# LoRA-conditioned projection and routed LoRA FFN: the setup's order of loads, copies and constant passes, and the banks of the last tile

## The chip, the cores and the metric

The kernel runs on one core of a Trainium2 chip. The metric is the device time of one execution in microseconds (us). The core's engines are TensorE (PE in the profile, its weight loads PEld), VectorE (DVE), ScalarE (ACT), GpSimd (POOL) and SyncE (SP), which in this kernel only issues DMAs.

## The reference

All data are float32. x is 8 batches of 512 rows of 2048. Each batch has an adapter (itok, one of 32) of rank 16. The result is x plus a routed low-rank FFN of a conditioned projection of x:

```python
# conditioned projection, per batch b
base_out = jnp.einsum('bti,oi->bto', x, W) + b
lora_h = jnp.einsum('bti,bir->btr', x, lora_As[adapter_mapping])
lora_out = jnp.einsum('btr,bro->bto', lora_h, lora_Bs[adapter_mapping])
y = base_out + lora_out * 2.0
# FFN: one of 8 experts per row, the one with the largest logit
logits = jnp.einsum('bsd,ed->bse', y, route_w)
topk_v, topk_idx = jax.lax.top_k(logits, 1)
route_weight = jax.nn.one_hot(topk_idx[..., 0], 8) * topk_v
h = jnp.einsum('bsd,erd->bser', y, A)
out = jnp.einsum('bser,eor->bso', route_weight[..., None] * h, Bw)
return x + out
```

W is 2048 by 2048 (16 MB in float32), x 32 MB, each batch's adapter two matrices of 16 by 2048.

## The kernel before

The projection y is never formed. What the FFN needs of y are 136 numbers a row (8 experts of rank 16, and 8 logits), so the kernel first folds W into the 136 columns `proj` (A and route_w side by side) and then applies the folded matrix to x. It has two stages.

**Setup.** W comes in 16 tiles of 128 output rows (1 MB each, `load_w`, four buffers), and proj in parts (`load_pj`). For each tile, `chunk_w` rearranges it into two halves `wv` of eight 128-column blocks: ScalarE copies the first half, VectorE the second (line 281). Each half has two buffers. Then `load_w(oc + 4)` is issued into the tile's buffer. `fold_w` adds the tile's 16 products into six PSUM banks `pc` (line 292): 16 float32 matmuls, each of which is two passes in the trace. After the last tile, ScalarE and VectorE alternately copy the banks to `cm` (line 302).

Beside the fold the setup makes the low-rank parts. `load_adapters` (line 159) works out the rows of each batch's adapters with small VectorE operations and fetches them through GpSimd's queue: `ad_b` (1 MB, one indirect DMA), `ad_ar` (1 MB, four indirect DMAs) and the bias. `turn_adapters` transposes `ad_b` on TensorE in four groups, ScalarE copies each (line 320); `turn` transposes `ad_ar` on VectorE (line 234); `fold_bias` forms the bias products on VectorE; `project_bias` and `project_adapters` are small matmuls, and the latter sends its result to DRAM and reads it back in four DMAs into `g4`.

The first unit of x (two tiles of 128 rows, 2 MB, `load_x`) is rearranged by `shuffle` into `xq` in 16 copies of 32 partitions (line 249): ScalarE makes four and GpSimd twelve. VectorE then transposes it in 32 by 32 blocks into `xT` (`turn_x`, line 234), and `heads` (line 400) can begin.

Before any of this, twelve matmuls on a constant tile `warm` run on TensorE (line 131). They read `warm` after a one-column ScalarE copy within the same tile (line 128), which in turn follows ScalarE's table load.

**Tile loop.** 32 tiles of 128 rows. In each half step n, TensorE does half of a tile's `heads`, and two of the four 512-column products of an earlier tile (`delta`, line 466). In between come `add_low` (the adapter's and the bias's part, line 424) and `turn_heads` (a transpose, line 455). VectorE does `route` (the choice of the expert, lines 437 to 445), `turn_low`, the next tile's transposes and `add_delta` (x plus the product, in place, line 478), after which SyncE stores the rows. ScalarE copies `whT` and seven of a unit's sixteen copies, GpSimd the rest.

The PSUM pools of the loop are `ps_h` (two tiles `ph`, 152 columns each), `ps_o` (two tiles `po` of two banks each) and `ps_s` (two).

**What sets the order.** The order on every engine is the order in which the program issues its instructions; the loop over `oc` (line 348) and the loop over n (line 509) write it out by hand. All loads and stores of W, proj, ffn_b and x stand in SyncE's queue, in program order, and a DMA in it that waits holds up those behind it.

Of the kernel before, what the change touches and what calls it, by code (L numbers as in the profile page):

```python
# [9 lines left out]
F32 = mybir.dt.float32  # L10
# [8 lines left out]
def kernel(  # L19
# [29 lines left out]
    nc = tc.nc  # L49
# [34 lines left out]

    warm = const.tile([P, P], F32, name="warm")
    nc.vector.memset(warm, 1.0)


    it_i = const.tile([P, B], I32, name="it_i")
# [27 lines left out]
    def load_x(u):  # L117
        xt = xpools[u % XB].tile([P, TPU, D], F32, tag=f"x{u % XB}", name=f"x_{u}")
        for k in range(TPU):
            b, r = divmod(TPU * u + k, TPB)  # L120
            nc.sync.dma_start(out=xt[:, k, :], in_=x[b, ts(r, P), :])
        x_tiles[u] = xt
# [2 lines left out]
    ident = const.tile([P, P], F32, name="ident")  # L125
    make_identity(nc, ident)

    nc.scalar.copy(warm[:, 1:2], warm[:, :1])
    pm = ps_s.tile([P, P], F32, tag="s", name="pm")
    for _ in range(12):  # L130
        nc.tensor.matmul(pm, warm, warm, start=True, stop=True)

    own_i = const.tile([P, B], I32, name="own_i")
# [22 lines left out]
    fb = const.tile([P, D], F32, name="fb")  # L156
    bias_o = const.tile([P, NO], F32, name="bias_o")

    def load_adapters():

        it_f = const.tile([P, B], F32, name="it_f")
        nc.vector.tensor_scalar(it_f, it_i, float(R), None, ALU.mult)
        row_f = const.tile([P, B], F32, name="row_f")
        nc.vector.tensor_tensor(row_f, it_f, own, ALU.add)
        nc.vector.tensor_tensor(row_f, row_f, mask, ALU.mult)
        brow_f = const.tile([P, 1], F32, name="brow_f")
        nc.vector.tensor_reduce(brow_f, row_f, AX.X, ALU.add)
        brow_i = const.tile([P, 1], I32, name="brow_i")
        nc.vector.tensor_copy(brow_i, brow_f)
        nc.gpsimd.indirect_dma_start(  # L170
            out=ad_b,
            out_offset=None,
            in_=cond_b,
            in_offset=bass.IndirectOffsetOnAxis(ap=brow_i, axis=0),
        )

        quad = const.tile([P, B], F32, name="quad")
        nc.vector.tensor_copy(quad, quad_i.rearrange("p i h -> p (i h)"))
        nc.vector.tensor_tensor(quad, quad, mask, ALU.mult)
        base = const.tile([P, 1], F32, name="base")  # L180
        nc.vector.tensor_reduce(base, quad, AX.X, ALU.add)
        odd = const.tile([P, 1], F32, name="odd")
        nc.vector.tensor_reduce(
            odd, mask.rearrange("p (i h) -> p h i", h=2)[:, 1, :], AX.X, ALU.add
        )
        it_q = const.tile([P, NQ, 2], F32, name="it_q")
        nc.vector.tensor_scalar(
            it_q, it_f.rearrange("p (k h) -> p k h", h=2), float(NQ), None, ALU.mult
        )
        arow_f = const.tile([P, NQ], F32, name="arow_f")  # L190
        nc.vector.tensor_tensor(arow_f, it_q[:, :, 1], it_q[:, :, 0], ALU.subtract)
        nc.vector.tensor_scalar(arow_f, arow_f, odd, base, ALU.mult, ALU.add)
        nc.vector.tensor_tensor(arow_f, arow_f, it_q[:, :, 0], ALU.add)
        arow_i = const.tile([P, NQ], I32, name="arow_i")
        nc.vector.tensor_copy(arow_i, arow_f)
        for m in range(NQ):
            nc.gpsimd.indirect_dma_start(
                out=ad_ar[:, m, :],
                out_offset=None,
                in_=cond_a.rearrange("s (i d) -> (s i) d", i=NQ),  # L200
                in_offset=bass.IndirectOffsetOnAxis(ap=arow_i[:, m : m + 1], axis=0),
            )
        nc.gpsimd.dma_start(out=bias_o, in_=bias)

    one = const.tile([P, NQ, Q], F32, name="one")
    own4 = const.tile([P, NQ], F32, name="own4")
# [25 lines left out]
    def turn(dst, src, h):  # L232

        nc.vector.transpose(  # L234
            dst[:, ts(h, HJ), :].rearrange("p j (g t) -> p g j t", t=Q),
            src.rearrange("p g (j a) -> p g j a", a=Q)[:, :, ts(h, HJ), :],
        )
# [69 lines left out]
    def fold_bias(js):  # L307
        for j in js:
            if j == 0:
                nc.vector.tensor_scalar(bp, pj[:, 0, :], bias_o[:, :1], None, ALU.mult)  # L310
            else:
                nc.vector.scalar_tensor_tensor(
                    bp, pj[:, j, :], bias_o[:, j : j + 1], bp, ALU.mult, ALU.add
                )

    def turn_adapters(g):
        pt = ps_s.tile([P, 4, P], F32, tag="s", name=f"pbT_{g}")
        for k in range(4):
            nc.tensor.transpose(pt[:, k, :], ad_b[:, ts(4 * g + k, P)], ident)
        nc.scalar.copy(ad_bT[:, ts(g, 4), :], pt)  # L320
# [27 lines left out]
    for oc in range(NO):  # L348
        if oc + 1 < NO:
            chunk_w(oc + 1)  # L350
        fold_w(oc)
        if oc == 2:
            load_adapters()
            fill_constants()
        if oc == 6:
            nc.sync.dma_start(out=fb, in_=ffn_b)
        if oc in (8, 10):
            load_x((oc - 8) // 2)
        if 6 <= oc < 10:
            turn_adapters(oc - 6)  # L360
        if oc in (7, 8):
            turn(ad_aT, ad_ar, oc - 7)
        if oc in (9, 10):
            fold_bias(range(8 * (oc - 9), 8 * (oc - 8)))
        if oc == 11:
            project_bias()
            project_adapters()
        if oc == 12:
            load_x(2)
            shuffle(0, moves[:4], nc.scalar.copy)  # L370
            shuffle(0, moves[4:], nc.gpsimd.tensor_copy)
        if oc == 13:
            for b in range(2):
                nc.scalar.copy(cm[:, :, ds(b * NA, R)], ad_aT[:, :, ts(b, R)])
        if oc == 14:
            for h in range(2):
                turn_x(0, h)
# [17 lines left out]
    def heads(t, j0, j1):  # L395
        s = batch_of(t) % 2
        if j0 == 0:
            ph_tiles[t] = ps_h.tile([P, NA], F32, tag="h", name=f"ph_{t}")
        for j in range(j0, j1):
            nc.tensor.matmul(  # L400
                ph_tiles[t],
                xT_tiles[t][:, j, :],
                cm[:, j, ds(s * R, NA)],
                start=(j == 0),
                stop=(j == NJ - 1),
            )
# [54 lines left out]

    def delta(t, h):

        po = ps_o.tile([P, HN, 512], F32, tag="o", name=f"po_{t}_{h}")
        for k in range(HN):
            nc.tensor.matmul(  # L466
                po[:, k, :], whT_tiles[t], fb[:, ts(h * HN + k, 512)], start=True, stop=True
            )
        po_tiles[t, h] = po

    def add_delta(t, h, parts=1):
        u, k = divmod(t, TPU)
        po = po_tiles.pop((t, h)).rearrange("p n d -> p (n d)")
        n = D // 2 // parts
        for m in range(parts):
            cols = ds(h * D // 2 + m * n, n)
            xs = x_tiles[u][:, k, cols]
            nc.vector.tensor_tensor(xs, xs, po[:, ts(m, n)], ALU.add)  # L478
            if t == NT - 1:
                store(t, cols)  # L480
        if t == NT - 2:
            store(t, ts(h, D // 2))
        elif t < NT - 2 and h == 1:
            store(t, ds(0, D))
# [24 lines left out]
    for n in range(2 * NT + 4):  # L509
        t, h = divmod(n, 2)  # L510
        if t < NT:

            if n == 3:
                heads(t, HJ, HJ + HJ // 2)
                turn_heads(0)
                heads(t, HJ + HJ // 2, NJ)
            else:
                heads(t, h * HJ, (h + 1) * HJ)
            if n == 2:
                add_low(0)  # L520
        if h == 0 and 0 < t <= NT:
            route(t - 1)
        tp, hp = piece(n - 1)
        if tp >= 0:
            add_delta(tp, hp, HN if tp == NT - 1 else 1)
        turn_x(t + 1, h)
        if h == 1 and 0 < t <= NT:
            keep_heads(t - 1)
        u, ms = shuffle_slot(n)
        shuffle(u, ms, nc.gpsimd.tensor_copy if n == 2 else nc.scalar.copy)  # L530
        if h == 1 and t < NT:
            turn_low(t)
        if piece(n)[0] >= 0:
            delta(*piece(n))
        if h == 1 and 0 < t < NT:
            add_low(t)
        if h == 1 and t < NT:
            b, k = divmod(t, TPB)
            if k == 0 and 0 < b < B - 1:
                nc.gpsimd.tensor_copy(  # L540
                    cm[:, :, ds((b + 1) % 2 * NA, R)], ad_aT[:, :, ts(b + 1, R)]
                )
        if h == 0 and 1 < t <= NT:
            turn_heads(t - 1)
        tq, hq = piece(n - 5)
        u, k = divmod(tq, TPU)
        if tq >= 0 and hq == 1 and k == TPU - 1 and u + XB < NU:
            load_x(u + XB)
# [48 lines left out]
```

## Time and profile before

| What | Value |
|---|---|
| median of 3 runs | 338.13 us (338.06 to 338.48) |
| profiled execution, own time | 338.08 us |
| its span, first to last instruction | 336.3 us |
| mean granted TensorE clock | 0.996 |
| TensorE busy | 324.2 us (96%) |
| VectorE busy | 232.3 us (69%) |
| ScalarE busy | 169.7 us (50%) |
| GpSimd busy | 138.1 us (41%) |
| DMA | 88.83 MB, 264 GB/s over the span |
| tile loop's first matmul | 75.58 us |

In a line of the timeline the first number is the start in us from the span's start, the second the time until the merged group's end; then come engine, line of the kernel, operation, output and inputs, and the count; in brackets the idle time of the engine before it, and what ended it. In a line of the chain of waits there are start, length and the work. In a line of the stretches, the stretch is followed by its length, then busy time and count of PE, PEld, DVE, ACT and POOL, then granted clock, the busy share of the DMA engines, and GB/s.

### The profile page before, as it was taken

Reading aid. Unit: us, or ns where it says so; the run is one execution under the profiler, and the core shown is the slowest. Engines: PE = TensorE matmul, PEld = TensorE weight load, DVE = VectorE, ACT = ScalarE, POOL = GpSimd, SP = SyncE. Lnnn points to the kernel's source line nnn. Section 1 sums busy time; section 2 is a strip of 40 time slices with the busy share of each in tenths; the row PEclk is TensorE's granted clock in tenths of the full one; section 3 lists DMA queues with packets and bytes.
Section 4 is the critical chain, followed back from the end, with each engine's and each line's share of the span. In section 5 each row is a group of like instructions: output and inputs, shape, how many; then the busy total and the mean of one; then the engine's idle time right before and its main releaser. Section 6 shows DMA issues by size and latency. Waiting matters only on the chain.

```text
span 336.3 us, 5099 instructions
## 1 busy us (share of the span) xinstructions
PE 324.2 (96%) x1962; PEld 259.9 (77%) x1962; DVE 232.3 (69%) x421; ACT 169.7 (50%) x193; POOL 138.1 (41%) x145
## 2 busy tenths in 40 slices
PE   6998999999999999999999999999999999999993
PEld 6898999998777777777777777777777777777751
DVE  1151464255887877787878787877877787877753
ACT  3222433625757566576647565757566575730000
POOL 2050001999981807182616455344708081700000
PEclk9999999999999999999999999999999999999998
DMA  7999999869333394949485766759494949333336
GB/s 218 401 405 411 413 417 420 333 239 399 147 128 139 126 370 196 385 153 383 141 359 179 323 223 276 264 239 342 172 374 170 377 160 385 146 125 127 126 125 250
DMA packets 15656, 88.83 MB, mean 264 GB/s; under 512 B 1664, under 2 KB 4368, under 8 KB 5392
## 3 DMA queue, kind: packets, MB, share of 16 engines
q1 hardware_dynamic: 14960, 86.33, 65.4%
q0 software_dynamic: 528, 2.11, 1.9%
q8 instruction: 15, 0.25, 0.3%
q10 hardware_dynamic: 144, 0.07, 0.1%
q14 instruction: 9, 0.07, 0.1%
HBM read 54.88 MB, written 33.62 MB: 263 GB/s over the span
## 4 chain that ended last, share of the span: by engine, by line
PE 77%; DMA 12%; POOL 4%; DVE 2%; issue 1%; ACT 1%; SPq 1%; DVEq 0%; POOLq 0%; ACTq 0%
PE ph L400 39%; PE po L466 32%; DMA w<-in_w_dram 8%; DMA x<-in_x_dram 4%; POOL xq L249 4%; PE pc L292 2%; PE ph L424 2%; PE pw L455 1%; ACT wv L281 1%; DVE xT L234 1%; DVE x L478 1%; DVE cm L302 0%; SPq L101 0%; DVE rw L443 0%; SPq L95 0%
## 5 line engine op out<-in xcount | busy, mean ns | idle before, releaser
L249 POOL COPY xq<-x 32x1024 f32<-32x1024 f32 x123 | 128.5, 1045 | 135.2 <-DMA x<-in_x_dram 102.2
L249 ACT COPY xq<-x 32x1024 f32<-32x1024 f32 x133 | 138.7, 1043 | 20.5 <-DMA x<-in_x_dram 13.6
L400 PE MATMUL ph<-cm,xT 128*128 128x152 f32 x1024 | 142.7, 293 | 0.5 <-DVE cm L302 0.5
L400 PEld LDWEIGHTS ph<-cm,xT 128*128 128x128 f32 x1024 | 135.2, 190 | 9.3 <-issue 8.7
L466 PE MATMUL po<-fb,whT 128*128 128x512 f32 x256 | 120.2, 592 | 0.8 <-DVE x L478 0.8
L478 DVE TENSOR_TENSOR x<-x,po 128x1024 f32<-128x1024 f32 (+1 forms) x66 | 77.4, 1177 | 6.7 <-PE po L466 6.4
L234 DVE STREAM_TRANSPOSE xT<-xq 128x1024 f32<-128x1024 f32 x64 | 78.7, 1234 | 3.1 <-POOL xq L249 3.1
L466 PEld LDWEIGHTS po<-fb,whT 128*128 128x128 f32 x256 | 44.8, 190 | 32.1 <-issue 31.1
L292 PE MATMUL pc<-pj,wv 128*128 128x136 f32 x512 | 61.1, 280 | 2.0 <-ACT wv L281 2.0
L292 PEld LDWEIGHTS pc<-pj,wv 128*128 128x128 f32 x512 | 60.0, 190 | 2.6 <-ACT wv L281 2.6
L460 ACT COPY whT<-pw 128x128 f32<-128x128 f32 x32 | 8.5, 266 | 90.1 <-PE pw L455 90.1
L281 DVE COPY wv<-w 128x1024 f32<-128x1024 f32 (+1 forms) x17 | 12.5, 739 | 33.6 <-DMA w<-in_w_dram 25.6
L281 ACT COPY wv<-w 128x1024 f32<-128x1024 f32 (+1 forms) x17 | 16.8, 996 | 30.6 <-DMA w<-in_w_dram 25.3
L437 DVE TENSOR_REDUCE top<-ph 128x1 f32<-128x8 f32 x32 | 5.3, 167 | 38.5 <-PE ph L424 38.5
L424 PEld LDWEIGHTS ph<-g,hT 128*128 128x128 f32 x64 | 12.1, 190 | 14.8 <-issue 12.2
L443 DVE TENSOR_SCALAR rw<-rank,win,top 128x8 f32<-128x8 f32 x32 | 16.4, 513 | 1.2
L424 PE MATMUL ph<-g,hT 128*128 128x136 f32 x64 | 12.6, 279 | 0.0
L455 PEld LDWEIGHTS pw<-ident,wh 128*128 128x128 f32 x32 | 4.5, 140 | 8.7 <-issue 5.5
L419 DVE STREAM_TRANSPOSE hT<-hls 128x128 f32<-128x128 f32 x32 | 10.0, 311 | 1.1
L445 DVE TENSOR_TENSOR wh<-ph,rw 128x128 f32<-128x128 f32 x32 | 9.3, 291 | 1.1
L455 PE MATMUL pw<-ident,wh 128*128 128x128 f32 x32 | 8.8, 274 | 0.8 <-DVE wh L445 0.8
L412 DVE TENSOR_TENSOR hls<-ph,own 128x64 f32<-128x64 f32 x32 | 6.0, 187 | 3.3 <-issue 2.3
(60 smaller groups left out, 65.8 us busy)
## 6 DMA issues: line engine op xcount, KB each, us to landing
x<-in_x_dram SPq DMA_DIRECT2D x32, 1024.0 KB, 9.0
out_dram<-x SPq DMA_DIRECT2D x30, 1024.0 KB, 4.8
w<-in_w_dram SPq DMA_DIRECT2D x16, 1024.0 KB, 12.7
fb<-in_ffn_b_dram SPq DMA_DIRECT2D x1, 1024.0 KB
out_dram<-x SPq DMA_DIRECT2D x2, 512.0 KB
out_dram<-x SPq DMA_DIRECT2D x4, 256.0 KB, 2.6
pj<-in_proj_dram SPq DMA_DIRECT2D x2, 272.0 KB, 13.2
pj<-in_proj_dram SPq DMA_DIRECT2D x2, 136.0 KB, 8.8
```

Of the source, the lines that this page charges most:

```text
L234: nc.vector.transpose(dst[:, ts(h, HJ), :].rearrange("p j (g t) -> p g j t", t=Q), src.rearrange("p g (j a) -> p g j a", a=Q)[:, :, ts(h, ...
L249: copy(xq_tiles[u][ts(i, Q), :, g, :], x_tiles[u][ts(g, Q), :, ts(i, DQ)])
L281: copy(dst[:, ts(k, n)], wr[:, ds(h * HJ + k * n, n)])
L292: nc.tensor.matmul(pc[:, k, :], wv_tiles[oc, h][:, j, :], pj[:, oc, :], start=(oc == 0 and k == 0), stop=(oc == NO - 1), skip_group_check= ...
L400: nc.tensor.matmul(ph_tiles[t], xT_tiles[t][:, j, :], cm[:, j, ds(s * R, NA)], start=(j == 0), stop=(j == NJ - 1),)
L419: nc.vector.transpose(hT, h.rearrange("p g s -> p (g s)"))
L424: nc.tensor.matmul(ph_tiles[t][:, ds((1 - b % 2) * R, NP)], hT_tiles.pop(t), g4[:, b, :], start=False, stop=True, skip_group_check=True,)
L443: nc.vector.tensor_scalar(rw, rank, win, top, ALU.is_equal, ALU.mult)
L445: nc.vector.tensor_tensor(wh.rearrange("p (e r) -> p e r", r=R), ph[:, :ER].rearrange("p (e r) -> p e r", r=R), rw.unsqueeze(2).to_broadca ...
L455: nc.tensor.transpose(pw, wh_tiles.pop(t), ident)
L466: nc.tensor.matmul(po[:, k, :], whT_tiles[t], fb[:, ts(h * HN + k, 512)], start=True, stop=True)
L478: nc.vector.tensor_tensor(xs, xs, po[:, ts(m, n)], ALU.add)
```

## The change

- The constant matmuls read a tile that only VectorE writes; ScalarE's one-column copy gets a tile of its own. There are 14 of them in place of 12.
- `load_adapters` becomes two functions. `load_adapters_b` (its rows, the fetch of `ad_b`, the bias) is issued at oc 4 and `load_adapters_a` (its rows, the four fetches of `ad_ar`) at oc 7, in place of both at oc 2. `turn_adapters` moves from oc 6 to 9 to oc 8 to 11, the turn of `ad_ar` from 7 and 8 to 10 and 11, and `project_adapters` from oc 11 to 12.
- In SyncE's queue, ffn_b stood between the loads of W at oc 6, unit 0 of x at oc 8, unit 1 at oc 10 and unit 2 after the reads of g at oc 12. Now unit 0, ffn_b, unit 1 and unit 2 follow one another at oc 10, after the last load of W.
- Of unit 0's sixteen copies ScalarE makes six, two each at oc 12, 13 and 14, and GpSimd ten. The first two adapters are copied into `cm` by VectorE in place of ScalarE.
- A `ph` tile takes a whole PSUM bank. The last tile's first half of products goes to two such banks in place of a `ps_o` tile, and its two adds read one bank each.

```diff
+    warm_a = const.tile([P, 2], F32, name="warm_a")
+    nc.vector.memset(warm_a[:, :1], 1.0)
...
-    nc.scalar.copy(warm[:, 1:2], warm[:, :1])
+    nc.scalar.copy(warm_a[:, 1:2], warm_a[:, :1])
     pm = ps_s.tile([P, P], F32, tag="s", name="pm")
-    for _ in range(12):
+    for _ in range(14):
         nc.tensor.matmul(pm, warm, warm, start=True, stop=True)
...
-    def load_adapters():
-
-        it_f = const.tile([P, B], F32, name="it_f")
+    it_f = const.tile([P, B], F32, name="it_f")
+
+    def load_adapters_b():
+
         nc.vector.tensor_scalar(it_f, it_i, float(R), None, ALU.mult)
...
+        nc.gpsimd.dma_start(out=bias_o, in_=bias)
+
+    def load_adapters_a():
 
         quad = const.tile([P, B], F32, name="quad")
...
-        nc.gpsimd.dma_start(out=bias_o, in_=bias)
...
         if oc == 2:
-            load_adapters()
             fill_constants()
-        if oc == 6:
-            nc.sync.dma_start(out=fb, in_=ffn_b)
-        if oc in (8, 10):
-            load_x((oc - 8) // 2)
-        if 6 <= oc < 10:
-            turn_adapters(oc - 6)
-        if oc in (7, 8):
-            turn(ad_aT, ad_ar, oc - 7)
+        if oc == 4:
+            load_adapters_b()
+        if oc == 7:
+            load_adapters_a()
+        if 8 <= oc < 12:
+            turn_adapters(oc - 8)
         if oc in (9, 10):
             fold_bias(range(8 * (oc - 9), 8 * (oc - 8)))
+        if oc == 10:
+            load_x(0)
+            nc.sync.dma_start(out=fb, in_=ffn_b)
+            load_x(1)
+            load_x(2)
+        if oc in (10, 11):
+            turn(ad_aT, ad_ar, oc - 10)
         if oc == 11:
             project_bias()
+        if oc == 12:
             project_adapters()
-        if oc == 12:
-            load_x(2)
-            shuffle(0, moves[:4], nc.scalar.copy)
-            shuffle(0, moves[4:], nc.gpsimd.tensor_copy)
+            shuffle(0, moves[6:], nc.gpsimd.tensor_copy)
+        if oc in (12, 13, 14):
+            shuffle(0, moves[2 * (oc - 12) : 2 * (oc - 11)], nc.scalar.copy)
         if oc == 13:
             for b in range(2):
-                nc.scalar.copy(cm[:, :, ds(b * NA, R)], ad_aT[:, :, ts(b, R)])
+                nc.vector.tensor_copy(cm[:, :, ds(b * NA, R)], ad_aT[:, :, ts(b, R)])
...
-            ph_tiles[t] = ps_h.tile([P, NA], F32, tag="h", name=f"ph_{t}")
+            ph_tiles[t] = ps_h.tile([P, 512], F32, tag="h", name=f"ph_{t}")[:, :NA]
...
-        po = ps_o.tile([P, HN, 512], F32, tag="o", name=f"po_{t}_{h}")
+        if (t, h) == (NT - 1, 0):
+
+            po = [ps_h.tile([P, 512], F32, tag="h", name=f"po_{t}_{k}") for k in range(HN)]
+        else:
+            po = ps_o.tile([P, HN, 512], F32, tag="o", name=f"po_{t}_{h}")
         for k in range(HN):
             nc.tensor.matmul(
-                po[:, k, :], whT_tiles[t], fb[:, ts(h * HN + k, 512)], start=True, stop=True
+                po[k] if isinstance(po, list) else po[:, k, :],
...
-    def add_delta(t, h, parts=1):
+    def add_delta(t, h):
         u, k = divmod(t, TPU)
-        po = po_tiles.pop((t, h)).rearrange("p n d -> p (n d)")
-        n = D // 2 // parts
-        for m in range(parts):
+        po = po_tiles.pop((t, h))
+        if t < NT - 1:
+            parts = [po.rearrange("p n d -> p (n d)")]
+        else:
+            parts = po if isinstance(po, list) else [po[:, m, :] for m in range(HN)]
+        n = D // 2 // len(parts)
+        for m, part in enumerate(parts):
             cols = ds(h * D // 2 + m * n, n)
             xs = x_tiles[u][:, k, cols]
-            nc.vector.tensor_tensor(xs, xs, po[:, ts(m, n)], ALU.add)
+            nc.vector.tensor_tensor(xs, xs, part, ALU.add)
```

More of the change, by code (lines that the diff above doesn't have):

```diff
@@ L462, in delta @@
     def delta(t, h):
-        po = ps_o.tile([P, HN, 512], F32, tag="o", name=f"po_{t}_{h}")
+        if (t, h) == (NT - 1, 0):
+            po = [ps_h.tile([P, 512], F32, tag="h", name=f"po_{t}_{k}") for k in range(HN)]
+        else:
+            po = ps_o.tile([P, HN, 512], F32, tag="o", name=f"po_{t}_{h}")
         for k in range(HN):
             nc.tensor.matmul(
-                po[:, k, :], whT_tiles[t], fb[:, ts(h * HN + k, 512)], start=True, stop=True
+                po[k] if isinstance(po, list) else po[:, k, :],
+                whT_tiles[t],
+                fb[:, ts(h * HN + k, 512)],
+                start=True,
+                stop=True,
             )
         po_tiles[t, h] = po
-    def add_delta(t, h, parts=1):
+    def add_delta(t, h):
         u, k = divmod(t, TPU)
-        po = po_tiles.pop((t, h)).rearrange("p n d -> p (n d)")
-        n = D // 2 // parts
-        for m in range(parts):
+        po = po_tiles.pop((t, h))
[5 more added lines that the diff above has]
+        for m, part in enumerate(parts):
             cols = ds(h * D // 2 + m * n, n)
             xs = x_tiles[u][:, k, cols]
-            nc.vector.tensor_tensor(xs, xs, po[:, ts(m, n)], ALU.add)
+            nc.vector.tensor_tensor(xs, xs, part, ALU.add)
             if t == NT - 1:
@@ L524 @@
         if tp >= 0:
-            add_delta(tp, hp, HN if tp == NT - 1 else 1)
+            add_delta(tp, hp)
         turn_x(t + 1, h)
```

## The prediction

> **What bounds the kernel now.** I read the page first, then the chain of waits, then the timeline of TensorE alone over the first 90 us, the stretches of DMA, and the last 12 us.
>
> ```profile
> PE 324.2 (96%) x1962; PEld 259.9 (77%) x1962; DVE 232.3 (69%) x421; ACT 169.7 (50%) x193; POOL 138.1 (41%) x145
> ```
>
> TensorE is busy for 96% of the span. Its waits say where anything can be won: none of its groups has a wait between 85 and 327 us, so the tile loop (228 us) is bound by its own matmuls. Only the setup before 75.58 us and the last tile are open. The timeline of TensorE in the setup:
>
> ```profile
> 11.73 15.13 PE L292 MATMUL pc<-pj,wv 128*128 128x136 f32 x128 [0.73 <-ACT wv L281]
> 27.76 3.97 PE L292 MATMUL pc<-pj,wv 128*128 128x136 f32 x32 [0.91 <-ACT wv L281]
> 32.07 3.97 PE L292 MATMUL pc<-pj,wv 128*128 128x136 f32 x32 [0.33 <-ACT wv L281]
> ...
> 60.11 14.99 PE L292 MATMUL pc<-pj,wv 128*128 128x136 f32 x128
> 75.58 6.44 PE L400 MATMUL ph<-cm,xT 128*128 128x152 f32 x48 [0.48 <-DVE cm L302]
> ```
>
> Folding W is 16 chunks of 3.71 us (the last four: 14.99 us, less a tail of 0.16, over 4). Chunks 5 and 6, at 27.76 and 32.07, waited for W. Second, the chain before the tile loop starts, whose columns are start, length and work:
>
> ```profile
> 43.07 14.64 DMA x<-in_x_dram
> ...
> 70.82 1.05 POOL xq L249
> 71.90 2.37 DVE xT L234 x2
> 74.27 1.18 DVE cm L302 x3
> 75.58 6.44 PE ph L400 x48
> ```
>
> TensorE's folding ends at 74.94 (75.10 with its tail), but the second chain ends at the same place: unit 0 of x lands at 57.7, GpSimd copies it until 71.86, VectorE turns it until 74.27, and then makes its three copies of cm. Two paths are tied here, and shortening one alone wins next to nothing. Third, what sets that landing. In the stretches, the last number is GB/s:
>
> ```profile
> 0.00:37.75 37.75, 33.08 (x265) 32.47 (x266) 9.83 (x36) 10.53 (x12) 7.19 (x16) 1.00 0.97 364
> 0.00:57.70 57.70, 53.03 (x438) 52.42 (x439) 22.21 (x60) 18.26 (x21) 7.19 (x16) 1.00 0.98 383
> 40.00:62.00 22.00, 22.00 (x193) 22.00 (x192) 12.03 (x24) 10.86 (x12) 3.99 (x4) 1.00 1.01 418
> ```
>
> The DMA engines are full from the first loads to 65 us. A transfer lands when all that is queued ahead of it, and about 1.06 MB more, has moved: by 57.7 us 22.10 MB (0.383 x 57.7) had moved, and x_0 and everything ahead of it is 14 tiles of W (14.68), proj (1.11), adapters (2.10), ffn_b (1.05) and x_0 (2.10), 21.04 MB. At the landing of w_8 (37.75 us, 13.74 MB moved against 12.65) the difference is 1.09, so the rule holds along the queue.
>
> **The change, part by part.** The sum is made against the profiled run, 338.08 us with a span of 336.3; it lies 0.05 us under the median of the three runs, 338.13.
>
> *Constant passes.* They start when VectorE's memset ends (0.84 + 0.17 us), not after ScalarE's table load and copy (2.65). In the trace 24 passes run from 2.71 to 7.1, at 4 in half a microsecond until 6.0 and 6 to 7 after it. So 28 passes from about 1.15 end near 6 us if the slow time lasts the same 3.4 us, at 7.6 if it lasts throughout. Chunk 0 could start at 6.4 in place of 7.13. But chunk 1 starts at 11.73 because w_1 lands at 10.6 and its copy takes 1.05 us, and nothing here moves w_1. Chunk 0 has 0.73 us to spare, which covers even a late end. Value 0.
>
> *Adapters later.* The 14 small VectorE operations (0.15 to 0.46 us each) stay the same work; five now follow the copy of w_5 and nine that of w_8, and the adapters' B is issued on GpSimd's queue near 25 us, A near 37 to 41. With 2.1 MB gone from the queue at 18.7 us, w_5 lands when 7.40 + 1.06 MB have moved: 5.21 MB by 16.8 us, then 409 GB/s, gives 24.8 us in place of 26.66, and w_6 27.3 in place of 30.9. With 1.1 us for the copy both are in time for 26.7 and 30.4, so both waits go. From 11.73 to 74.94 is 63.2 us; the work in it is 15 x 3.71, four transposes of adapters of 0.44, pb 0.23 and pg 3.71, which is 61.3. Between 1.6 (the two restarts against 26.69 and 31.5) and 1.9 us come free: folding ends near 73.2.
> What is late next: in the trace B and A got 2.1 MB in 19.5 us (issued from 18.73, last landing 38.2), 108 GB/s beside W. A alone then lands at 47 to 49. VectorE reaches the turn of A near 49.6, with the copy of w_12 queued behind it, which TensorE needs at 56.5; a landing up to 54.5 costs nothing. B lands near 35, its first transpose is at 41.5.
>
> *SyncE's order.* Now all of W, then x_0, ffn_b, x_1, x_2, all issued between 48 and 51 us. Ahead of and with x_0 are 16 x 1.049 + 1.11 + 2.10 + 2.10 = 22.09 MB, plus 1.06 is 23.15. That is 1.05 MB past the 22.10 of before, at 418 GB/s: x_0 lands at 60.2, **2.5 us later**. The engines do not run dry on the way, since at each new load of W 0.9 MB or more is still to move. The write of g to DRAM now queues behind x_2: it lands near 73 (before at 67.97, where the reads of it began), the four reads near 77.5; the first use is at 81.9, so 4 us cover them. ffn_b lands at 62.7, first used at 85.3. x_2 lands sooner than 75.3 (69.76 + 5.5), but its copies come after 84: nothing.
>
> *Sharing unit 0.* GpSimd makes 10 copies in place of 12, ScalarE 6 in place of 4 (around its W copies; it would end near 69 us, behind nobody). A row of GpSimd alone and one beside a VectorE copy:
>
> ```profile
> 60.03 1.03 POOL L249 COPY xq<-x 32x1024 f32<-32x1024 f32 x1
> 61.11 1.40 POOL L249 COPY xq<-x 32x1024 f32<-32x1024 f32 x1
> ```
>
> Two copies fewer are -2.14 us (1.07 start to start). Three of the twelve were 0.37 longer, each beside a VectorE copy of W; two such remain, so -0.37. The two cm copies go from ScalarE (0.40 each) to VectorE. No row shows them there: 0 each if they fall between, 0.37 each if each meets a copy; for a quarter of the elements I take 0.2 each, +0.4. Together -2.1.
> The Trainium skill (SBUF, "two separate sides") speaks against this move: VectorE copies and GpSimd hold one shared port pair exclusively, each for a whole instruction, the other being blocked. By that rule a W copy would cost GpSimd its whole length; the row shows 0.37 for a copy whose undisturbed row is 0.69. The row decides; by the rule the cost would be some 0.3 us a W copy higher, before as after.
>
> So GpSimd ends at 60.2 + 0.19 + 10.7 + 0.74 + 0.4 = 72.2 (before 71.86). Behind it stand the same 3.72 us (turns, three cm copies, start): the tile loop starts at 75.9 to 76.0, **+0.4 us**. The 1.7 us of TensorE are lost in that wait.
>
> *The last tile.*
>
> ```profile
> 326.66 0.27 ACT L460 COPY whT<-pw 128x128 f32<-128x128 f32 x1 [5.58 <-PE pw L455]
> 327.33 3.67 PE L466 MATMUL po<-fb,whT 128*128 128x512 f32 x8 [0.76 <-DVE x L478]
> 329.32 1.28 DVE L478 TENSOR_TENSOR x<-x,po 128x512 f32<-128x512 f32 x2 [1.01 <-PE po L466]
> ```
>
> The first product of the last tile waits until VectorE has emptied its banks (327.19); with banks of the heads' pool it waits for whT alone, 326.93 plus 0.12: 327.05, **-0.28 us**. All eight passes follow without a wait and the closing adds and stores hang on their end. The bounds are 0 and -0.4 (start at 326.93). Splitting the first half's adds moves stores that are not last. The wider bank of each ph tile touches a loop in which TensorE never waits: 0.
>
> Sum: 0 + 0.4 - 0.28 = +0.1 on 338.08: **338.2 us**, which is no change. Its own ends: landing of x_0 +-0.4, cm copies -0.4 or +0.35, last tile +0.28 or -0.12, and the route of tile 0, where TensorE waits 0.85 us for VectorE and the step rw took 0.80 (0.29 to 1.00 elsewhere in the loop), -0.5 or +0.2. Not all fall on one side: 337.2 to 339.0.
>
> **The rivals.**
> *x_0 comes in time (faster).* The tie breaks for TensorE: folding ends at 73.2 to 73.4 and the loop starts 0.64 later, at 74.0, with the last tile 338.08 - 1.6 - 0.28 = 336.2. It needs x_0 by 58.3. For it: adapters got only a quarter of the rate beside W; whatever of them is unmoved when x_0 moves brings x_0 forward, 2.5 us a MB. Against it: by 108 GB/s nothing is left after 49 us.
> *TensorE's clock falls (slower).* TensorE would idle from 73.2 to 76.0; the longest gap in the fold was 0.91 us, so the trace has no such case. The price is that of the start: 3.4 us at 0.23 us a pass in place of 0.107 loses 1.8 us, giving 340.0. It decides if a gap of 2.7 us is enough to slow the passes.
> The Trainium skill (TensorE: Matmul & The Clock Gate, "The HAM clock gate") puts the idle window at about 3.4 us, by which this gap costs 0; no run here shows it.
> *A wait in ScalarE or VectorE (slower).* ScalarE now waits for x_0 ahead of the copy of w_14: it reaches TensorE late if x_0 lands after 62.6; VectorE waits for A ahead of w_12, late after 54.5. A landing 1.5 us past either gives 339.7.
>
> **How the numbers follow.** Likeliest case 0.55 (0.06 faster, 0.43 within, 0.06 slower), x_0 in time 0.25 (0.23 faster, 0.02 within), clock 0.10, wait 0.06, some other gain 0.04 (0.03 faster, 0.01 within): faster 0.32, same 0.46, slower 0.22. 0.2% is 0.68 us, about what a measurement of this kernel tells from no change. The range 336.1 to 339.2 leaves out the clock case, most of the wait case and the lower edge of the first rival, some 0.2 together.
>
> **What would show it.** Right: chunks 1 to 8 without a wait and folding ending near 73.3; x_0 landing at 59.8 to 60.6; GpSimd's tenth copy ending at 71.8 to 72.6; the first ph matmul near 75.9 after 2 us or more of idle, released through VectorE; whT to the last po in 0.1 us. Wrong: a landing of x_0 before 59, ph before 75, slow passes after the gap, or a wait of pc on wv after 40 us.

## The result, and the profile after

The changed kernel took 337.25 us (median of 22 runs, 336.34 to 339.1) beside 337.94 us for the kernel before (22 runs, 337.29 to 338.48). The ratio is 0.9984 with a 95% interval of 0.9973 to 0.9994: a gain of 0.2 to 0.9 us, 0.54 by the ratio. That is inside the forecast range (336.1 to 339.2) and within the 0.2% that was called no change, but the interval is clear of one, and the forecast point, 338.2, lay 0.1 us on the other side. The runs spread unevenly: four of the 22, at 337.9 to 339.1 us, had a mean granted TensorE clock of 0.991 to 0.994, the others 0.995 or more, and a median of 337.2.

The line of busy times from the page of the changed kernel, and TensorE's timeline in its setup:

```profile
PE 324.5 (97%) x1966; PEld 260.3 (78%) x1966; DVE 233.4 (70%) x424; ACT 171.1 (51%) x193; POOL 136.0 (41%) x143
```

```profile
1.06 5.12 PE L133 MATMUL pm<-warm 128*128 128x128 f32 x28 [1.06 <-DVE warm_a L88]
6.31 3.97 PE L297 MATMUL pc<-pj,wv 128*128 128x136 f32 x32
11.85 29.92 PE L297 MATMUL pc<-pj,wv 128*128 128x136 f32 x256 [1.56 <-ACT wv L286]
...
62.13 11.28 PE L297 MATMUL pc<-pj,wv 128*128 128x136 f32 x96
75.19 6.44 PE L409 MATMUL ph<-cm,xT 128*128 128x152 f32 x48 [1.78 <-DVE cm L307]
```

The constant passes start at 1.06 and chunk 0 at 6.31, but chunk 1 still waits for the copy of w_1 and starts at 11.85. From there chunks 1 to 8 run without a wait (256 passes in one piece), and folding ends at 73.41 with its tail, 1.7 us sooner than before. Then TensorE waits 1.78 us. The chain of waits says for what:

```profile
48.82 11.04 DMA x<-in_x_dram
...
60.02 1.03 POOL xq L254
...
70.44 1.05 POOL xq L254
71.51 2.37 DVE xT L239 x2
73.88 1.17 DVE cm L307 x3
75.19 6.44 PE ph L409 x48
```

Unit 0 of x lands at 59.86 (57.7 before), GpSimd's ten copies end at 71.49 (twelve at 71.86 before), and the same two steps of VectorE follow. In the last tile the first product starts 0.05 us after `whT` is copied; it had waited 0.40 for VectorE:

```profile
326.26 0.27 ACT L469 COPY whT<-pw 128x128 f32<-128x128 f32 x1 [5.58 <-PE pw L464]
326.58 3.70 PE L479 MATMUL po<-fb,whT 128*128 128x512 f32 x8 [0.41 <-ACT whT L469]
330.32 1.28 DVE L499 TENSOR_TENSOR x<-x,po 128x512 f32<-128x512 f32 x2 [1.03 <-PE po L479]
```

### The profile page after: what moved, and what is told of

Read it like the earlier page. It is cut to its first block, busy times and chain, and to the rows that moved or that the text cites. A ratio compares the mean times of both kernels' runs of the same rounds, so it can differ in the third digit from the quotient of the medians.

```text
span 335.4 us, 5111 instructions
## 1 busy us (share of the span) xinstructions
PE 324.5 (97%) x1966; PEld 260.3 (78%) x1966; DVE 233.4 (70%) x424; ACT 171.1 (51%) x193; POOL 136.0 (41%) x143
## 4 chain that ended last, share of the span: by engine, by line
PE 86%; DMA 6%; POOL 3%; DVE 2%; issue 1%; ACT 1%; SPq 0%; DVEq 0%; POOLq 0%; ACTq 0%
PE ph L409 39%; PE po L479 33%; PE pc L297 10%; DMA x<-in_x_dram 3%; POOL xq L254 3%; DMA w<-in_w_dram 3%; PE ph L433 2%; PE pw L464 1%; DVE xT L239 1%; ACT wv L286 1%; DVE cm L307 0%; PE pbT L324 0%; DVE rw L452 0%; SPq L103 0%; DVE x L499 0%
## 5 line engine op out<-in xcount | busy, mean ns | idle before, releaser
L254 POOL COPY xq<-x 32x1024 f32<-32x1024 f32 x121 | 125.9, 1041 | 122.6 <-DMA x<-in_x_dram 80.7
L254 ACT COPY xq<-x 32x1024 f32<-32x1024 f32 x135 | 140.8, 1043 | 23.8 <-DMA x<-in_x_dram 16.7
L452 DVE TENSOR_SCALAR rw<-rank,win,top 128x8 f32<-128x8 f32 x32 | 15.6, 488 | 1.2
L173 POOL DMA_INDIRECT raw<-in_cond_b_dram,brow_i x1 | 1.0, 1031 | 23.5 <-DVE brow_i L172 23.5
```

The source lines that it names most:

```text
L254: copy(xq_tiles[u][ts(i, Q), :, g, :], x_tiles[u][ts(g, Q), :, ts(i, DQ)])
L452: nc.vector.tensor_scalar(rw, rank, win, top, ALU.is_equal, ALU.mult)
```

## The experiments

Eleven kernels ran, one of them twice, in three groups. Each group had its own runs of the kernel before: 337.82 us in the first (21 runs: the setup alone, the last tile alone, x_0 after w_13, ffn_b first), 338.06 in the second (20: the adapters early twice, `cm` on ScalarE, the filled gap), 338.04 in the third (17: the others). Most single executions of it lie within half a microsecond of these, some up to 1.7 us over, so two terms of 0.3 us can't be told apart by times; the profiles serve for that.

### The setup alone, and the last tile alone

The first kernel is the changed one with `delta`, `add_delta` and the `ph` tiles of before:

```diff
-            ph_tiles[t] = ps_h.tile([P, 512], F32, tag="h", name=f"ph_{t}")[:, :NA]
+            ph_tiles[t] = ps_h.tile([P, NA], F32, tag="h", name=f"ph_{t}")
...
-        if (t, h) == (NT - 1, 0):
-            po = [ps_h.tile([P, 512], F32, tag="h", name=f"po_{t}_{k}") for k in range(HN)]
-        else:
-            po = ps_o.tile([P, HN, 512], F32, tag="o", name=f"po_{t}_{h}")
+        po = ps_o.tile([P, HN, 512], F32, tag="o", name=f"po_{t}_{h}")
```

> The changed kernel with the last tile's banks and the ph tiles as before. Theory (two independent gains: the tile loop starts 0.4 us sooner because x_0's copies end sooner, and the last tile loses its wait of about 0.35 us): 0.4 us under the kernel before, the tile loop starting at 75.2, the last tile's first product 0.4 to 0.5 us after whT again. Rival (the gain is in the last tile alone, and the start at 75.19 in the one profile is within what single executions scatter): no difference from the kernel before.

Measured: 337.59 us, ratio 0.9995 (0.9984 to 1.0007). The second kernel is the reverse, these lines of the change on the kernel before:

> The kernel before with only the ph tiles' whole banks and the last tile's first half in them. Theory: 0.35 us under the kernel before, all of it between whT and the first product of the last tile; start of the tile loop at 75.6. Rival: no difference, if the wait taken away returns behind the matmuls, in VectorE's last adds or the stores.

Measured: 337.81 us, ratio 0.9998 (0.9989 to 1.0007). Neither part is clear of no change by itself; by time, both rivals stand. The profiles settle one of them. From the first `ph` matmul to the end of the add with which VectorE follows TensorE's last matmul (the last work in the chain of waits; one more add ends 0.6 us after it in every profile) takes 256.15 us in the kernel before and 256.14 in the setup alone, 255.82 in the changed kernel and 255.81 in the last tile alone. The first line is the setup alone, the second the last tile alone:

```profile
326.84 3.67 PE L475 MATMUL po<-fb,whT 128*128 128x512 f32 x8 [0.76 <-DVE x L487]
```

```profile
326.59 3.70 PE L470 MATMUL po<-fb,whT 128*128 128x512 f32 x8 [0.41 <-ACT whT L460]
```

So the last tile is worth 0.33 us, and it does not come back later. The setup's part stays at 0.2 us by the ratio, from a gain of 0.5 to a loss of 0.2. The last tile alone also shows something not looked for. Its setup is that of the kernel before, instruction for instruction, but TensorE ran the fold of chunks 1 to 6 without a wait, and x_0 landed at 57.09 (42.02 + 15.07):

```profile
12.21 22.78 PE L292 MATMUL pc<-pj,wv 128*128 128x136 f32 x192 [0.77 <-ACT wv L281]
...
75.21 6.44 PE L400 MATMUL ph<-cm,xT 128*128 128x152 f32 x48 [1.16 <-DVE cm L302]
```

The two waits for W at 27.76 and 32.07 are thus not in every execution of the old setup, nor is the tie: here x_0's path ended last by itself, and the tile loop started at 75.21 with the old order, as it did at 75.19 with the new one.

### x_0 sooner, x_0 later

Unit 0 of x ahead of the last two tiles of W:

```diff
+        if oc == 8:
+            load_x(0)
         if oc == 10:
-            load_x(0)
             nc.sync.dma_start(out=fb, in_=ffn_b)
```

> The changed kernel with unit 0 of x put in SyncE's queue after w_13 (oc 8), ahead of w_14 and w_15; ffn_b and units 1 and 2 stay at oc 10. Theory (the landing of x_0, and GpSimd's ten copies behind it, set the start of the tile loop, and a landing comes when all bytes queued ahead have moved): x_0 lands 5 us sooner, near 55, GpSimd ends near 67, TensorE's own folding becomes the last path (end at 73.3) and the tile loop starts near 74.0: 1.2 us under the changed kernel, 1.9 under the kernel before. Rival (the fold, or the copies of W behind it, are what ends last): no gain over the changed kernel, or a loss, since w_14 and w_15 land 5 us later.

Measured: 335.94 us, ratio 0.9934 (0.992 to 0.9947). Run once more in the third group:

> The kernel with x_0 after w_13 once more, beside the one with w_1 in quarters. Theory: 1.9 us under the kernel before, as in its first run, near 336.0.

Measured: 335.87 us, ratio 0.9937 (0.9915 to 0.996). TensorE's wait before the tile loop is now that for its own last chunk (first kernel):

```profile
62.14 11.28 PE L297 MATMUL pc<-pj,wv 128*128 128x136 f32 x96
73.91 6.44 PE L410 MATMUL ph<-cm,xT 128*128 128x152 f32 x48 [0.48 <-DVE cm L307]
```

GpSimd started its ten copies at 54.85 in place of 60.02. That is the landing rule's 5 us for two MB. The opposite, ffn_b ahead of x_0:

```diff
-            load_x(0)
             nc.sync.dma_start(out=fb, in_=ffn_b)
+            load_x(0)
             load_x(1)
```

> The changed kernel with ffn_b ahead of unit 0 of x in SyncE's queue. Theory (each MB ahead of x_0 is 2.5 us of landing, and the path behind it has no slack): x_0 lands near 62.4, the tile loop starts near 77.7, 2.5 us over the changed kernel, 1.8 over the kernel before. ScalarE's copy of w_14 stands behind x_0's copies and just makes it. Rival (the engines take the transfers side by side, or GpSimd has slack): under 1 us over the changed kernel.

Measured: 341.52 us, ratio 1.01 (1.0085 to 1.0116), 3.7 us over the kernel before. x_0 landed at 61.84 and the tile loop started at 77.26, 2.07 us later than in the changed kernel. The rest was not expected: the first 48 passes took 9.23 us in place of 6.44. The stretches of this kernel (the granted clock is the number after POOL's count):

```profile
77.26 9.23 PE L409 MATMUL ph<-cm,xT 128*128 128x152 f32 x48 [3.93 <-DVE cm L307]
```

```profile
77.30:83.00 5.70, 5.70 (x23) 5.70 (x24) 2.08 (x2) 1.61 (x2) 5.49 (x6) 0.50 1.00 415
83.00:86.00 3.00, 3.00 (x25) 3.00 (x25) 0.54 (x2) 0.00 (x0) 2.86 (x4) 1.00 0.92 388
```

After 3.93 us without work the clock stood at 0.50 for more than 5 us. (In the trace's record of the clock it was 0.50 from 76.14 to 82.97: it fell 2.8 us into the gap.) To tell cause from company, the gap was filled, with everything else alike:

```diff
+    pm = ps_s.tile([P, P], F32, tag="s", name="pm_gap")
+    for _ in range(16):
+        nc.tensor.matmul(pm, warm, warm, start=True, stop=True)
     wctx.close()
```

> The kernel with ffn_b ahead of x_0, and 16 more constant matmuls (32 passes, 3.4 us) between the fold and the tile loop, whose product nobody reads. Theory (TensorE's granted clock fell to 0.50 in the 3.9 us in which it had nothing to do, and stayed there for 5 us): the clock stays at 1.00, the first 48 passes of ph take 6.4 us in place of 9.2, and the time is 2.3 to 2.8 us under the unfilled kernel, near 339. Rival (these passes are slow for something else that comes with the late landing): 9.2 us again and no gain.

Measured: 339.8 us, ratio 1.0053 (1.0039 to 1.0067), 1.7 us under the unfilled kernel as medians, 1.6 by the ratios, which is less than the 2.3 expected. The passes are back to their length:

```profile
73.38 3.73 PE L389 MATMUL pm_gap<-warm 128*128 128x128 f32 x32
77.77 6.44 PE L412 MATMUL ph<-cm,xT 128*128 128x152 f32 x48 [0.66 <-DVE cm L307]
```

So the idle time makes the passes slow. The add behind the last matmul ended 1.8 us sooner in the profile with the filled gap (333.59 against 335.37), although x_0 landed 0.51 later there (62.35).

### When the adapters are fetched

```diff
         if oc == 2:
+            load_adapters_b()
+            load_adapters_a()
             fill_constants()
-        if oc == 4:
-            load_adapters_b()
-        if oc == 7:
-            load_adapters_a()
```

> The changed kernel with both fetches of adapters at oc 2 again, everything else as changed. Theory (the late fetch lets TensorE fold W without waits, but the path of x_0 ends later, so the fold's gain is hidden): x_0 lands near 59.9 as in the changed kernel, since the same bytes lie ahead; folding ends 1.0 to 1.9 us later, at 74.3 to 75.1, the tile loop starts at 75.2 to 75.8: 0 to 0.6 us over the changed kernel. Rival (the changed kernel's gain comes from the waits for W that it takes away): 1.5 us or more over it.

Measured: 337.15 us, ratio 0.9978 (0.9968 to 0.9989), no slower than the changed kernel (0.9984). x_0 landed at 59.75: the same bytes lay ahead of it. The fold had one small wait again, and its end moved by 0.3 us, less than expected:

```profile
11.59 18.80 PE L297 MATMUL pc<-pj,wv 128*128 128x136 f32 x160 [1.22 <-ACT wv L286]
30.59 11.50 PE L297 MATMUL pc<-pj,wv 128*128 128x136 f32 x96 [0.20 <-ACT wv L286]
...
75.09 6.44 PE L407 MATMUL ph<-cm,xT 128*128 128x152 f32 x48 [1.36 <-DVE cm L307]
```

The same edit on the kernel with x_0 after w_13:

> The kernel with x_0 after w_13 and, in addition, both fetches of adapters at oc 2 again. Theory: with x_0 early TensorE's fold ends last, so the waits for W now count in full: 1.0 to 1.9 us over the kernel with x_0 after w_13, that is near 337.4, 0.4 under the kernel before. Rival (the late fetch is worth nothing anywhere): no difference from the kernel with x_0 after w_13.

Measured: 336.45 us, ratio 0.9957 (0.9944 to 0.997). The intervals (0.9934 with 0.992 to 0.9947) touch; the difference is 0.8 us by the ratios and 0.5 by the medians, and the tile loop starts at 74.73 against 73.91 and 73.86. So by the profiles the late fetch counts where TensorE's own path ends last, at about 0.8 us rather than 1.0 to 1.9; by time alone this isn't clear of no difference. Where x_0's path ends last, no gain of it is seen.

### Sharing the work on unit 0

The two copies of the first adapters into `cm` back on ScalarE:

```diff
-                nc.vector.tensor_copy(cm[:, :, ds(b * NA, R)], ad_aT[:, :, ts(b, R)])
+                nc.scalar.copy(cm[:, :, ds(b * NA, R)], ad_aT[:, :, ts(b, R)])
```

> The changed kernel with the two first copies into cm on ScalarE, as before. Theory (VectorE's two copies take 1.1 us each because they wait for GpSimd, and cost GpSimd nothing: its ten copies took 11.46 us, eight of 1.07 and two of 1.44 beside copies of W): no difference in GpSimd's ten copies nor in the time, within 0.3 us. Rival, the prediction's term (each costs GpSimd about 0.2 us): 0.4 us under the changed kernel, ten copies in about 11.0 us.

Measured: 337.35 us, ratio 0.998 (0.9969 to 0.9991), like the changed kernel. GpSimd's ten copies ran from 59.96 to 71.43, 11.47 us, against 60.02 to 71.49. In the changed kernel VectorE's two copies took 1.1 us each, yet the GpSimd copies beside them have their plain length. VectorE's rows, then the chain's rows of GpSimd, both of the changed kernel:

```profile
62.54 1.21 DVE L286 COPY wv<-w 128x1024 f32<-128x1024 f32 x1
63.67 2.20 DVE L383 COPY cm<-ad_aT 128x256 f32<-128x256 f32 x2
66.03 1.31 DVE L286 COPY wv<-w 128x1024 f32<-128x1024 f32 x1 [0.16 <-PE pc L297]
```

```profile
63.24 1.40 POOL xq L254
64.69 1.03 POOL xq L254
65.76 1.04 POOL xq L254
```

The copy that met w_14's took 1.40; the two that met those of `cm` took 1.03 and 1.04. It is VectorE that waits: singly its `cm` copies end at 64.80 and 65.87, each about 0.15 after a GpSimd copy. The first and last of the ten with `cm` on ScalarE:

```profile
59.96 1.03 POOL xq L254
...
70.38 1.05 POOL xq L254
```

The traces also show why the small copies are free. In the setups of the 14 profiles 30 GpSimd copies were lengthened, by 0.37 to 0.56 us, each beside a copy of W, and every one ended 0.89 to 0.90 us after VectorE's copy had ended. A plain copy takes 1.03. So VectorE's work costs GpSimd only what of it reaches beyond the first 0.14 us of GpSimd's own copy: a waiting copy of W reaches 0.51 in and costs 0.37, one of `cm` reaches 0.11 in and costs nothing.

And unit 0 shared twelve to four, as many as before:

```diff
-            shuffle(0, moves[6:], nc.gpsimd.tensor_copy)
-        if oc in (12, 13, 14):
+            shuffle(0, moves[4:], nc.gpsimd.tensor_copy)
+        if oc in (12, 13):
```

> The changed kernel with unit 0's copies shared 12 to GpSimd and 4 to ScalarE (two each at oc 12 and 13), as many as before. Theory (GpSimd's copies stand on the path from x_0 to the tile loop, at 1.07 us each): the tile loop starts 2.1 us later, near 77.3; TensorE then idles for 3.9 us after its fold, in which the clock fell in the kernel with ffn_b first, so 2.1 to 4.9 us over the changed kernel, 339.3 to 342. Rival (ScalarE's last copies end last, or GpSimd is not on the path): under 0.5 us.

Measured: 340.76 us, ratio 1.0081 (1.0051 to 1.011), within the 339.3 to 342 expected. x_0 landed where it did (59.87), and the tile loop started 2.19 us later, after a wait of 3.86, with the clock at 0.74 in 77.2 to 80.0 us and 0.68 in 80.0 to 83.0:

```profile
77.38 8.11 PE L409 MATMUL ph<-cm,xT 128*128 128x152 f32 x48 [3.86 <-DVE cm L307]
```

```profile
77.20:80.00 2.80, 2.62 (x15) 2.65 (x16) 2.31 (x3) 1.89 (x2) 2.72 (x3) 0.74 0.98 413
80.00:83.00 3.00, 3.00 (x17) 3.00 (x17) 0.00 (x0) 0.00 (x0) 2.88 (x4) 0.68 1.00 415
```

In the record of the clock that is 0.50 from 78.53 to 81.94: here it fell 1.1 us after the passes had begun again.

### The first microseconds

The constant passes as before:

```diff
-    nc.scalar.copy(warm_a[:, 1:2], warm_a[:, :1])
+    nc.scalar.copy(warm[:, 1:2], warm[:, :1])
...
-    for _ in range(14):
+    for _ in range(12):
```

> The changed kernel with the constant matmuls as before: 12, on the tile that ScalarE's copy also writes. Theory (chunk 0 has time to spare, since chunk 1 waits for w_1, which lands at 10.7): chunk 0 starts near 7.1 in place of 6.3, chunk 1 near 11.8 as in the changed kernel, no difference in time within 0.3 us. Rival (an earlier start of TensorE is kept): 0.7 us over the changed kernel.

Measured: 337.51 us, ratio 0.998 (0.9966 to 0.9994), like the changed kernel. Chunk 0 started at 6.91, chunk 1 at 11.77. That left the wait of chunk 1 itself, which is on the path once x_0 is early. The copy of w_1 in quarters:

```diff
-            n = HJ // 2 if oc == 0 else HJ
+            n = HJ // 2 if oc < 2 else HJ
             for k in range(HJ // n):
-                copy = copies[1 - k] if oc == 0 else copies[h]
+                copy = copies[1 - k] if oc < 2 else copies[h]
```

> The kernel with x_0 after w_13, and the copy of w_1 split over both engines in quarters as that of w_0. Theory (with x_0 early, all of TensorE's fold is on the path, and its one wait left is that of chunk 1 for ScalarE's 1.05 us copy of w_1): chunk 1 starts 0.6 us sooner, near 11.2, the tile loop too, 0.4 to 0.6 us under the kernel with x_0 after w_13. Rival (the next tiles of W come too late for it): chunk 4 or 5 waits instead, no gain.

Measured: 335.58 us, ratio 0.9928 (0.9905 to 0.9951), beside 335.87 (0.9937) for the same kernel without it: not told apart by time. Chunk 1 started at 11.06 and the tile loop at 73.11, 0.75 sooner than beside it, but 0.82 was lost again in tile 0, in one step of the route. The first fence is w_1 in quarters, the second the kernel beside it:

```profile
73.11 6.44 PE ph L410 x48
...
80.47 1.13 DVE rw L453
```

```profile
73.86 6.44 PE ph L410 x48
...
81.23 0.30 DVE rw L453
```

TensorE waits for this step in tile 0. In the ten profiles with the new last tile and a clock that did not fall ahead of the tile loop, the time from the first `ph` matmul to the end of the add behind the last matmul is 255.02 us plus this step, to 0.01: from 255.31 with 0.29, over 255.82 with 0.80, to 256.13 with 1.12.

## Why the prediction was right or wrong

**What bounds the kernel: right.** Only the setup and the last tile moved; the loop between them did not.

**Constant passes and the wide bank, 0: right.** Chunk 0 was sooner, chunk 1 not; undoing the constant passes changed nothing, and the loop of the kernels with the wide bank differs from that of the others by 0.32 us, the last tile's gain.

**Adapters later, folding 1.6 to 1.9 us sooner, hidden: right in the result, wrong in the size.** The landings came as forecast (w_5 at 24.45 for 24.8, w_6 at 26.93 for 27.3). Folding did end 1.7 us sooner between the two profiles and TensorE did lose it waiting for x_0. But the waits that it was to remove stood in one execution. In another of the same setup they were missing, and with the early fetch put back into the changed kernel only 0.3 us returned, 0.8 with x_0 early. A's landing was late by a little (50.07, where 47 to 49 was forecast): VectorE waited 0.51 us for it until 50.19, which the cover took.

**x_0 2.5 us later: right, and 0.3 too late in this profile.** The rule gave 60.2; measured were 59.86, and 59.75, 59.75, 59.80, 59.87 and 60.18 in five kernels with as many bytes ahead of it. The landing before was 57.7 in one profile and 57.09 in the other, so the shift is 2.2 to 2.8. The rule held in both directions: two MB fewer gave 5.2 us at GpSimd's start, one more gave 2.0 and, with the gap filled, 2.5.

**Sharing unit 0, -2.1: this is the term that failed.** Of it -2.14 and -0.37 were right; the +0.4 for the two `cm` copies on VectorE is 0: ten copies took 11.47 us with them on VectorE and 11.47 without. Forecast were 11.84 (10.7 + 0.74 + 0.4). Without this term the setup's +0.4 becomes about 0, and the last tile's gain is no longer cancelled. The lower bound that the prediction gave, 0 each, was the true one, but for another reason than falling between two copies: each did meet one. Scaling the cost of a copy of W by the elements was the error, because 0.14 us of VectorE's work costs nothing. Of the 0.7 to 0.8 us by which the profiled loop started ahead of the forecast 75.9 to 76.0, 0.37 is this term and 0.34 the landing, which is within the 0.4 allowed for it.

**The last tile, -0.28: right in the mechanism, 0.33 to 0.35 in size.** The first product starts 0.05 us after `whT`, not 0.12.

Put together: 0 for the setup and -0.33 gives 337.75 on 338.08. The measured ratio asks for 0.2 to 0.9 us, so this sum is inside, and its centre would be another 0.2. Whether the setup gains that 0.2 is open: the setup alone gave 0.2 with an interval on both sides of zero, and its starts of the tile loop (75.09 to 75.69 in five profiles) lie about those of the old order (75.58 and 75.21). In tile 0 the step `rw` gave nothing to either side in these profiles (0.80 before and after); it took up to 1.11 elsewhere in the trace before, not 1.00.

**The rivals.** "x_0 comes in time" did not happen in this kernel, but its price was right: with x_0 ahead of w_14 the loop started at 73.9 (forecast 74.0) and the time was 335.9 (forecast 336.2). "TensorE's clock falls" was not seen after the 1.78 us of the changed kernel's profile, nor after 2.35 with the old constant passes; it was after 3.86 and 3.93, and cost 1.7 and 2.8 us of passes where 1.8 was forecast. (That price was read from counts of passes that touch each half microsecond; at the start they begin 0.213 us apart until 6.07 and 0.111 after it, which makes it 1.6.) The prediction held that the trace had no such case, but each trace has one at its end: after the last pass the clock fell 2.9 us later in the kernel before, 2.1 in the changed one, and 2.1 to 4.5 in the 14 profiles. (The mean clock of 0.996 in both profiles is this end alone.) A gap of 2.35 us kept the clock and one of 2.1 lost it, so no fixed length decides, and the changed kernel's gap of 1.8 us is close to the shortest of these. The Trainium skill (TensorE: Matmul & The Clock Gate, "The HAM clock gate") has about 3.4 us for the idle window; these rows lie to both sides of it, and the measurement decides. Whether the clock fell ahead of the loop in other executions of the changed kernel isn't shown, as one trace of it was kept. It would fit the four of its 22 runs with a mean clock of 0.991 to 0.994, where the five of the kernel with ffn_b first had 0.988 to 0.993 and the 22 with x_0 early 0.995 or more. No wait of ScalarE or VectorE reached TensorE.

## What to carry to other kernels

Where two paths end together, find out which queue position sets the longer one before shortening the other. Here one more move in SyncE's queue, x_0 two places sooner, took the kernel from 0.5 us under the kernel before to 2.2 us under it, by the ratios.

The landing of a load in a full queue could here be forecast to about half a microsecond from bytes alone: all that is queued ahead, plus a constant that the same trace gives. A wait seen in one profile, by contrast, may belong to that execution; a second profile of the same program is worth having before its removal is counted as a gain.

## What the runs showed of the hardware

TensorE's granted clock fell to 0.50 in a gap of 3.93 us without work and just behind one of 3.86, and stayed there for 6.83 and 3.41 us. Sixteen unused matmuls in the gap kept it at 1.00 and made the kernel 1.7 us faster, though nobody reads their product. The fall does not come at a fixed time: 2.1 to 4.5 us after the last pass at the end of the 14 profiles, and once 1.1 us after the passes had begun again.

VectorE's copies beside GpSimd's wait for it, and it for them: a copy of 1024 elements a partition cost GpSimd 0.37 us where VectorE had waited, up to 0.56 where it had not, and one of 256 elements nothing, though it took VectorE 1.1 us. The Trainium skill (SBUF — State Buffer, "SBUF: two separate sides") has an exclusive lock that blocks the loser for a whole instruction; VectorE's 1.1 us agrees with that, and GpSimd's rows show 0.14 us less than the rule would cost it. In tile 0 the step `rw`, 8 elements a partition, took 0.29 to 1.12 us while GpSimd was copying; where it took longer than 0.29, it ended 0.03 us after a GpSimd copy, and each tenth of it was a tenth of the kernel's time.
